# The order of loads, sums and stores at the borders of two node loops in a graph layer (one core)

## Chip, core and metric

One core of a Trainium2 chip runs the whole layer. The metric is device time in microseconds (us), as the median of the runs of one kernel. The engines are PE (TensorE: matmuls and transposes into eight PSUM banks), DVE (VectorE), ACT (ScalarE), POOL (GpSimd) and SP (SyncE, which here only issues transfers). Each engine works through its own list of instructions.

## What is computed

There are 32 batches of 512 tokens with 256 channels, and one 512 x 512 adjacency matrix for each batch.

```python
h = maximum(layernorm(x), 0)
c1 = relu(bn1(conv1(h)));  x_conv = relu(h + bn2(conv17(c1)))      # 1 tap, then 17 taps along the tokens
s = h @ w_se.T + b_se                                                # 3 features of each token
A = exp(-|s_n - s_m|^2) * adj                                        # affinity, masked
msg = relu(h @ w_msg.T + b_msg);  x_nmp = A @ msg
gi = concat(x_conv, x_nmp) @ w_ih.T + b_ih;  gh = h @ w_hh.T + b_hh
r = sigmoid(gi_r + gh_r);  z = sigmoid(gi_z + gh_z);  n = tanh(gi_n + r * gh_n)
out = x + (1 - z) * n + z * h
```

All of it is float32.

## The kernel before

The batches form two groups of 16 (`GB`). Each group passes through two phases, and one late phase follows for all.

- **First phase** (`first_part`): it normalises a batch (`statistics`, `normalise`, which writes `xn`), transposes it (`transpose_h`, which writes `hT`, also stored to memory as `hd`), does the one-tap convolution (`conv1`, which writes `h1`) and turns windows of its result into frequencies (`windows_to_freq`, which writes `xf`). In group 0 the 17-tap weights are turned into frequencies as well and stored as `wd`.
- **Node phase** (`nodes`): it computes the affinity and the messages of every batch of the group, multiplies them, and between these does the frequency products (`product`) of the 17-tap convolution. This is the phase that the change touches.
- **Late phase**: for pairs of batches it goes back from frequencies (`inverse`), computes the gates with combined weights `sw` (`gates_rz`, `gate_n`), and writes the output.

The order of the instructions on every engine, and of the transfers on every queue, is the order in which the Python code makes the calls. Nothing reorders them (`tc.manual_schedule()`); only the waits between engines are put in by the framework, from the buffers that the calls read and write.

In the node phase the batches come in the order `todo`: the last of the group first, since its `hT` is still there, then the others. So group 0 has batches 15, 0, 1, ..., 14 and group 1 has 31, 16, ..., 30. For each batch:

- `load_adj` (L406) issues four transfers of 256 KB on SP; there are two buffers. `load_h` (L413) brings one `hT` of 512 KB back, and `by_chunks` (L424) puts it into another order with two ACT copies; the result is `hq`.
- `message` (L430) is 16 matmuls on PE (L442), with additions on DVE (L444, L445) and a ReLU on ACT. It gives the messages and the three features `st`.
- `features` (L450) writes the matrices `fl` and `fr` with six DVE instructions. `factors` (L460) transposes them on PE into `psl` and `psr` (L463, L468), and ACT copies them to `sl` and `sr`.
- `turn` (L472) transposes adjacency on DVE (L475), in four parts. `exponents` (L479) makes the distances `pd` on PE (L486) and the exponentials on ACT (L488). `masked` (L490) multiplies the two on DVE (L492).
- `aggregate7` (L527) forms the product of messages and affinity with seven half-size products (L538) where a plain one needs eight. For that POOL adds and subtracts blocks: `affinity_sums` (L499, four instructions of 128 x 512, results in `ts`) and `message_sums` (L508, four of 128 x 256, results in `ms`). The second of the seven products reads the third result of the first and the second of the other, called t2 and s2. There is one buffer for `ts` and one for `ms`. The last two batches of group 1 use the plain product (`aggregate`, L517, L522). ACT and DVE collect the result in `nmp`, of which there is one buffer, and `save_nmp` (L560) stores it through ACT's queue.
- `multiply(u)` does the product of frequency unit `u`: `product` (L372, matmuls L390 in three pairs, copies and additions of the result `y`), whose store is put into the list `stores` and sent by the next `flush()`; then `prepare` of unit u + 2, which makes the operands of its third pair with two POOL additions (`wsum`, L357, and `both`, L370); then the load of one further unit (`load_unit`, L351, two transfers on SP). There are three buffers for unit weights. The units are spread over the iterations: two or three in each of group 0, about three in each of the first 13 of group 1, none in the last three of group 1.

Before its loop, `nodes` does the messages, features and affinity of the first batch and the messages and features of the second. An iteration `i` then multiplies batch `todo[i]` with its affinity and gets `todo[i+1]` (`more[0]`), `todo[i+2]` and `todo[i+3]` ready.

Of the kernel before, what the change touches and what calls it, by code (L numbers as in the profile page):

```python
# [15 lines left out]
P = 128  # L16
# [49 lines left out]
def gnn_layer(  # L66
# [283 lines left out]
    def load_unit(g, u, pool=wts):  # L350
        t = WT[g, u] = pool.tile([P, 2, DC, D], FP, tag="wt", name=f"wt_{g}_{u}")  # L351
        for k in range(2):
            nc.sync.dma_start(t[:, k], WD[2 * u + k, : D * D].rearrange("(p i o) -> p i o", i=DC, o=D))
# [52 lines left out]
    def load_adj(b):  # L406
        ADJ[b] = pools["nodes"].tile([P, N // 32, P], FP, tag="adj", name=f"adj_{b}", bufs=2)

        rows = adj[b].rearrange("(j r) (g m) -> g r j m", r=32, g=4)
        for g in range(4):  # L410
            nc.sync.dma_start(ADJ[b][32 * g : 32 * (g + 1)], rows[g])
# [60 lines left out]
    def turn(b, mcs):  # L472
        for mc in mcs:
            at = AT[b, mc] = pools["nodes"].tile([P, N], FP, tag="at", name=f"at_{b}_{mc}", bufs=2)
            nc.vector.transpose(at.rearrange("p (j k) -> p j k", k=32), ADJ[b][:, :, 32 * mc : 32 * (mc + 1)])  # L475
        if NC - 1 in mcs:
            del ADJ[b]
# [36 lines left out]
        nc.gpsimd.tensor_tensor(t[:, 1], a21, a11, op=sub)  # L514
        nc.gpsimd.tensor_tensor(t[:, 2], a12, t[:, 1], op=sub)

    def aggregate(b):  # L517
        NMP[b] = work.tile([P, DC, N], FP, tag="nmp", name=f"nmp_{b}", bufs=1)
        for dc in range(DC):
            p = bank(f"pn_{b}_{dc}")  # L520
            for mc in range(NC):
                nc.tensor.matmul(p, MSG[b][:, mc, dc * P : (dc + 1) * P], A[b][:, mc, :],  # L522
                                 start=(mc == 0), stop=(mc == NC - 1))
            nc.scalar.copy(NMP[b][:, dc, :], p)
        del MSG[b], A[b]

    def aggregate7(b):  # L527

# [471 lines left out]
    with tc.tile_pool(name="freq", bufs=1) as fpool:  # L1000
# [3 lines left out]
        with phase("first", "gen"):  # L1004
            gen = pools["gen"]
            per = N // D
            steps = [partial(weights_to_freq, gen, pc, i) for pc in range(QI // PI) for i in range(0, PI, per)]

            X[0] = pools["first"].tile([P, NC, D], FP, tag="x", name="x_0", bufs=3)
            for c in range(NC):  # L1010
                (nc.sync if c % 2 == 0 else nc.scalar).dma_start(X[0][:, c, :], x[0, c * P : (c + 1) * P, :])
            load_w1()
            load_x(1)
            load_taps(gen, 0, nc.sync)
            nc.scalar.dma_start(taps, nc.inline_tensor(taps_np, name="dft_taps").ap())
            nc.scalar.dma_start(fwd, nc.inline_tensor(fwd_np, name="dft_fwd").ap())

            def between(b):
                if 1 <= b <= len(load_weights):
                    load_weights[b - 1]()  # L1020

                n = (2, 0, *(3 if b in (6, 11) else 2 for b in range(2, GB)))[b]
                mine = [[steps.pop(0)] for _ in range(n)]
                if b % 2 == 0 and b // 2 + 1 < QI // PI:
                    mine[b > 0].insert(0, partial(load_taps, gen, b // 2 + 1))
                return (mine[0], mine[1:]) if b == 0 else mine

            with tc.manual_schedule():
                xf = first_part(0, freq_tile, between)

                for u in range(2):
                    load_unit(0, u)


        LEFT = 4

        def nodes(g, xf, units, last, following=()):


            b1 = (g + 1) * GB  # L1040
            pw = pools["pw"]
            todo = [b1 - 1] + list(range(g * GB, b1 - 1))
            loads = [u for u in (*units, *following) if (g, u) not in WT]
            stores = []

            def load_units(n):
                for _ in range(n):
                    if loads:
                        load_unit(g, loads.pop(0))

            def flush():
                while stores:
                    stores.pop(0)()

            def multiply(u):
                product(pw, g, u, xf, stores)
                if u + 2 in units:
                    prepare(pw, g, u + 2, xf)
                load_units(1)

            load_adj(todo[0])
            load_adj(todo[1])
            load_units(3 - sum((g, u) in WT for u in units))
            load_h(todo[3])
            message(todo[0])
            features(todo[0])
            message(todo[1], [0])
            factors(todo[0])
            message(todo[1], [1])
            turn(todo[0], [0, 1])  # L1070
            features(todo[1])
            exponents(todo[0])
            by_chunks(todo[2])
            masked(todo[0], [0, 1])
            turn(todo[0], [2, 3])
            masked(todo[0], [2, 3])
            affinity_sums(todo[0])
            prepare(pw, g, units[1], xf)
            for i, b in enumerate(todo):
                mine = spread(units, i, last) if i < last else []  # L1080
                more = todo[i + 1 : i + 5]
                seven = i <= last

                if g + 1 < NG and i == GB // 2:
                    load_x(b1)
                if g + 1 < NG and i == 3 * GB // 4:
                    statistics(b1)
                if len(more) > 1:
                    load_adj(more[1])
                if len(more) > 3:  # L1090
                    load_h(more[3])
                if seven:
                    message_sums(b)
                if more:
                    factors(more[0])
                flush()
                for u in mine[:1]:
                    multiply(u)
                if len(more) > 1:
                    message(more[1])  # L1100
                    flush()
                    features(more[1])
                if more:
                    turn(more[0], [0, 1])
                    exponents(more[0])
                    masked(more[0], [0, 1])
                for u in mine[1:2]:
                    multiply(u)
                if more:
                    turn(more[0], [2, 3])  # L1110
                    masked(more[0], [2, 3])
                if seven:
                    aggregate7(b)
                else:
                    aggregate(b)
                if more and i + 1 <= last:
                    affinity_sums(more[0])
                flush()
                for u in mine[2:]:
                    multiply(u)  # L1120
                save_nmp(b)
                if len(more) > 2:
                    by_chunks(more[2])
            flush()

        with phase("pw", "ahead"):
# [103 lines left out]
```

## Time and profile before

| | |
|---|---|
| Median of 3 runs | 1826.45 us (1826.16 to 1829.45) |
| The profiled execution | 1826.99 us |
| Its span, from the first to the last instruction | 1825.1 us |
| PE matmuls / weight loads, busy | 98% / 63% |
| DVE / POOL / ACT, busy | 66% / 43% / 34% |
| First phase of group 0 | to 156 us |
| Node phase of group 0 | 156 to 451 us |
| First phase of group 1 | 451 to 566 us |
| Node phase of group 1 | 566 to 859 us |
| Late phase | 859 us to the end |

The page gives busy times of the engines over the span; "granted clock" is the share of its full rate at which PE ran. A wait has the form "engine line waited for: us in total, times, longest", and in a timeline the brackets hold the idle time of the engine before the instruction and what ended it. A waiting instruction is named by the line of the call that issued it. DMA queues bear the name of the engine that issues on them.

### The profile page before, as it was taken

To read this page: it belongs to the slowest core of one execution; us is meant where nothing else is said; L and a number is where in the kernel's file an instruction comes from. 1 tells how busy PE (TensorE), PEld (TensorE's weight loads), DVE (VectorE), ACT (ScalarE), POOL (GpSimd) and SP (SyncE) were. 2 spreads that over 40 slices of the span, in tenths; PEclk is the share of its full clock that TensorE was granted. 3 is DMA by queue.
4 is the path that set the end of the run, shared out by engine and by line. 5 is a ranking of instruction groups with operands and counts; after the bars stand their busy time and mean duration, and the time that the engine had idled before them with its cause. 6 is when DMAs were issued, how large, how long until landed. Compare 5 with 4: busy or idle time off the path is not lost.

```text
span 1825.1 us, 21215 instructions
## 1 busy us (share of the span) xinstructions
PE 1793.3 (98%) x6974; PEld 1152.5 (63%) x6974; DVE 1203.6 (66%) x2370; ACT 617.9 (34%) x1252; POOL 781.1 (43%) x731
## 2 busy tenths in 40 slices
PE   9998999999999999999999999999999999999998
PEld 6776778887998888886545554555445554555444
DVE  7874877876896778774266556664666456655666
ACT  4554444443445444443212221222212221222121
POOL 3431787777433877776421332223231323133221
PEclk9998999999999999999999999999999999999999
DMA  9999786885668887888342244224422443234412
GB/s 260 309 293 226 209 243 202 247 222 175 218 231 214 238 240 233 235 227 269 81 119 69 55 121 121 87 35 121 121 89 40 114 121 101 54 88 121 117 21 53
DMA packets 308657, 289.32 MB, mean 159 GB/s; under 512 B 148076, under 2 KB 238732, under 8 KB 308164
## 3 DMA queue, kind: packets, MB, share of 16 engines
q1 hardware_dynamic: 282964, 225.79, 46.7%
q10 hardware_dynamic: 18992, 38.68, 6.0%
q0 software_dynamic: 6592, 23.50, 4.1%
q8 instruction: 56, 0.92, 0.2%
q14 instruction: 53, 0.43, 0.1%
HBM read 191.50 MB, written 96.40 MB: 158 GB/s over the span
## 4 chain that ended last, share of the span: by engine, by line
PE 92%; DVE 2%; POOL 2%; issue 2%; DMA 1%; ACT 0%; SPq 0%; ACTq 0%; DVEq 0%; POOLq 0%
PE pg L664 30%; PE pn L664 15%; PE py L390 11%; PE pn L538 9%; PE pm L442 6%; PE pc L326 6%; PE pc L652 5%; PE px L341 3%; PE pd L486 2%; PE pw L254 2%; PE phT L310 1%; DMA adj<-in_adj_dram 1%; PE pn L522 1%; PE pz L664 1%; PE psr L468 1%
## 5 line engine op out<-in xcount | busy, mean ns | idle before, releaser
L642 POOL TENSOR_TENSOR hp<-hp 128x512 f32<-128x512 f32 x64 | 80.5, 1269 | 415.1 <-DMA hp<-hd 352.3
L664 PE MATMUL pg<-hp,sw 128*128 128x512 f32 x434 | 221.8, 593 | 1.1 <-DVE u L695 0.6
L664 PE MATMUL pg<-np,sw 128*128 128x512 f32 x434 | 221.6, 592 | 0.0
L664 PE MATMUL pg<-cp,sw 128*128 128x512 f32 x434 | 221.6, 592 | 0.0
L642 POOL TENSOR_TENSOR cp<-cp 128x512 f32<-128x512 f32 x64 | 80.6, 1269 | 225.0 <-ACT cp L658 223.7
L390 PE MATMUL py<-wt,xf 128*128 128x256 f32 x640 | 157.0, 389 | 0.0
L679 ACT ACTIVATE rz<-rz,brz 128x512 f32<-128x512 f32 x93 | 67.0, 721 | 260.2 <-DVE rz L683 260.2
L664 PEld LDWEIGHTS pg<-hp,sw 128*128 128x128 f32 x434 | 82.2, 190 | 105.1 <-issue 97.4
L664 PEld LDWEIGHTS pg<-np,sw 128*128 128x128 f32 x434 | 82.5, 190 | 103.8 <-issue 103.8
L664 PEld LDWEIGHTS pg<-cp,sw 128*128 128x128 f32 x434 | 82.5, 190 | 103.8 <-issue 103.8
L357 POOL TENSOR_TENSOR wsum<-wt 128x512 f32<-128x512 f32 x78 | 107.6, 1380 | 83.3 <-DMA wt<-wd 57.7
L390 PEld LDWEIGHTS py<-wt,xf 128*128 128x128 f32 x640 | 118.6, 193 | 35.4 <-issue 21.2
L803 ACT ACTIVATE nt<-nt,vech 128x512 f32<-128x512 f32 x64 | 46.2, 722 | 236.5 <-DVE nt L802 236.5
L442 PE MATMUL pm<-wmsg,hq 128*128 128x259 f32 x512 | 119.1, 385 | 1.9 <-ACT hq L427 1.9
L326 PE MATMUL pc<-w,hT 128*128 128x256 f32 x512 | 117.7, 383 | 0.9 <-DVE hT L314 0.9
L664 PE MATMUL pn<-cp,sw 128*128 128x512 f32 x224 | 114.4, 592 | 0.0
L664 PE MATMUL pn<-np,sw 128*128 128x512 f32 x224 | 114.4, 592 | 0.0
L664 PE MATMUL pn<-hp,sw 128*128 128x512 f32 x224 | 114.4, 592 | 0.0
L326 PEld LDWEIGHTS pc<-w,hT 128*128 128x128 f32 x512 | 94.6, 190 | 23.9 <-issue 5.6
L492 DVE TENSOR_TENSOR A<-A,at 128x512 f32<-128x512 f32 x128 | 108.2, 882 | 1.9 <-ACT A L488 1.9
L442 PEld LDWEIGHTS pm<-wmsg,hq 128*128 128x128 f32 x512 | 97.0, 191 | 19.0 <-ACT hq L427 4.0
L652 PEld LDWEIGHTS pc<-back,yt 128*128 128x128 f32 x640 | 92.7, 190 | 7.7 <-issue 7.7
(169 smaller groups left out, 3379.1 us busy)
## 6 DMA issues: line engine op xcount, KB each, us to landing
wt<-wd SPq DMA_DIRECT2D x160, 256.0 KB, 4.9
adj<-in_adj_dram SPq DMA_DIRECT2D x128, 256.0 KB, 6.7
wd<-wst SPq DMA_DIRECT2D x64, 320.0 KB, 5.5
yd<-y ACTq DMA_DIRECT2D x80, 256.0 KB, 4.5
yt<-yd SPq DMA_DIRECT2D x30, 640.0 KB, 7.5
hd<-hT SPq DMA_DIRECT2D x32, 512.0 KB, 5.0
nd<-nmp ACTq DMA_DIRECT2D x32, 512.0 KB, 4.7
xb<-in_x_dram SPq DMA_DIRECT2D x128, 128.0 KB, 3.7
```

The lines of the kernel that those rows point to most:

```text
L326: nc.tensor.matmul(p[:, j, :], HT[b][:, ic, c * P : (c + 1) * P], w1[:, ic, :], start=(ic == 0), stop=(ic == DC - 1))
L341: nc.tensor.matmul(p[:, j * 2 * L : (j + 1) * 2 * L], H1[b][:, c0 + j, ic * P : (ic + 1) * P], fwd, start=True, stop=True)
L357: nc.gpsimd.tensor_tensor(t, WT[g, u][:, 0], WT[g, u][:, 1], op=ALU.add)
L390: nc.tensor.matmul(dst, v[:, ic, :], w[:, ic, :], start=(ic == 0), stop=(ic == DC - 1))
L442: nc.tensor.matmul(p[:, : D + NS], hq[:, ic, c * P : (c + 1) * P], wmsg[:, ic, :], start=(ic == 0), stop=(ic == DC - 1))
L492: nc.vector.tensor_mul(A[b][:, mc, :], A[b][:, mc, :], AT.pop((b, mc)))
L538: nc.tensor.matmul(bk, left[:, k, :], right[:, k, :], start=(first and k == 0), stop=(k == 1), skip_group_check=True)
L642: nc.gpsimd.tensor_tensor(t[:, dst, :], t[:, a, :], t[:, b, :], op=sub)
L652: nc.tensor.matmul(bk[:, t0:t1], YT[p][j][:, c, oc * P : (oc + 1) * P], back[:, n : n + t1 - t0], start=(c == 0), stop=(c == len(spans) - ...
L664: nc.tensor.matmul(bk[:, t], sw[:, k, q, o, :], terms[k][q][:, t], start=(first and i == 0), stop=(i == len(ks) - 1), skip_group_check=True)
L679: nc.scalar.activation(rz[:, g, j, :], src, AF.Sigmoid, bias=brz[:, g : g + 1], scale=1.0)
L803: nc.scalar.activation(n, n, AF.Tanh, bias=b_in[:, i : i + 1], scale=1.0)
```

## The change

- The loads of units 0 and 1 leave the end of group 0's first phase. `nodes` now issues the adjacency of its first batch, then three unit loads (in group 1 they are loaded already), then the second adjacency.
- Ahead of the loop, `message_sums` of the first batch comes right after its features; the features of the second batch and the exponentials of the first come before the first `turn`; `prepare` of the second unit comes before `affinity_sums`.
- In an iteration, `message_sums` of the next batch comes just before its `affinity_sums`, at the end, and no longer at the top of the iteration after. `by_chunks` moves from the end to the place after the exponentials. `save_nmp` is not called at once but put into `stores`, to be sent by the next `flush()`.
- In the first iteration alone, the message of batch `todo[2]` and its features (`bring`) come before the product of unit 0.
- In the last iteration, all units that are left are multiplied before the aggregation.
- A plain aggregation is split: its first half comes ahead of the next batch's `turn` and exponentials.

```diff
--- before.py
+++ after.py
@@ -514,15 +514,17 @@
         nc.gpsimd.tensor_tensor(t[:, 1], a21, a11, op=sub)
         nc.gpsimd.tensor_tensor(t[:, 2], a12, t[:, 1], op=sub)
 
-    def aggregate(b):
-        NMP[b] = work.tile([P, DC, N], FP, tag="nmp", name=f"nmp_{b}", bufs=1)
-        for dc in range(DC):
+    def aggregate(b, dcs=range(2)):
+        if 0 in dcs:
+            NMP[b] = work.tile([P, DC, N], FP, tag="nmp", name=f"nmp_{b}", bufs=1)
+        for dc in dcs:
             p = bank(f"pn_{b}_{dc}")
             for mc in range(NC):
                 nc.tensor.matmul(p, MSG[b][:, mc, dc * P : (dc + 1) * P], A[b][:, mc, :],
                                  start=(mc == 0), stop=(mc == NC - 1))
             nc.scalar.copy(NMP[b][:, dc, :], p)
-        del MSG[b], A[b]
+        if DC - 1 in dcs:
+            del MSG[b], A[b]
 
     def aggregate7(b):
 
@@ -1028,9 +1030,6 @@
             with tc.manual_schedule():
                 xf = first_part(0, freq_tile, between)
 
-                for u in range(2):
-                    load_unit(0, u)
-
 
         LEFT = 4
 
@@ -1059,27 +1058,34 @@
                 load_units(1)
 
             load_adj(todo[0])
+            load_units(3 - sum((g, u) in WT for u in units))
             load_adj(todo[1])
-            load_units(3 - sum((g, u) in WT for u in units))
             load_h(todo[3])
             message(todo[0])
             features(todo[0])
+            message_sums(todo[0])
             message(todo[1], [0])
             factors(todo[0])
             message(todo[1], [1])
-            turn(todo[0], [0, 1])
             features(todo[1])
             exponents(todo[0])
             by_chunks(todo[2])
+            turn(todo[0], [0, 1])
             masked(todo[0], [0, 1])
             turn(todo[0], [2, 3])
             masked(todo[0], [2, 3])
+            prepare(pw, g, units[1], xf)
             affinity_sums(todo[0])
-            prepare(pw, g, units[1], xf)
             for i, b in enumerate(todo):
                 mine = spread(units, i, last) if i < last else []
                 more = todo[i + 1 : i + 5]
                 seven = i <= last
+
+                def bring():
+                    if len(more) > 1:
+                        message(more[1])
+                        flush()
+                        features(more[1])
 
                 if g + 1 < NG and i == GB // 2:
                     load_x(b1)
@@ -1089,22 +1095,24 @@
                     load_adj(more[1])
                 if len(more) > 3:
                     load_h(more[3])
-                if seven:
-                    message_sums(b)
                 if more:
                     factors(more[0])
                 flush()
+                if i == 0:
+                    bring()
                 for u in mine[:1]:
                     multiply(u)
-                if len(more) > 1:
-                    message(more[1])
-                    flush()
-                    features(more[1])
+                if i > 0:
+                    bring()
+                if not seven:
+                    aggregate(b, [0])
                 if more:
                     turn(more[0], [0, 1])
                     exponents(more[0])
+                    if len(more) > 2:
+                        by_chunks(more[2])
                     masked(more[0], [0, 1])
-                for u in mine[1:2]:
+                for u in mine[1:2] if more else mine[1:]:
                     multiply(u)
                 if more:
                     turn(more[0], [2, 3])
@@ -1112,15 +1120,15 @@
                 if seven:
                     aggregate7(b)
                 else:
-                    aggregate(b)
+                    aggregate(b, [1])
+                flush()
+                stores.append(partial(save_nmp, b))
                 if more and i + 1 <= last:
+                    message_sums(more[0])
                     affinity_sums(more[0])
-                flush()
-                for u in mine[2:]:
-                    multiply(u)
-                save_nmp(b)
-                if len(more) > 2:
-                    by_chunks(more[2])
+                if more:
+                    for u in mine[2:]:
+                        multiply(u)
             flush()
 
         with phase("pw", "ahead"):
```

## Prediction

> **What bounds the kernel now.** I read the page's busy row first: TensorE (PE) is busy 98% of the span, so only its 32 us of holes, and the stretches at half clock that follow holes, can be won. The chain of waits confirms it (PE 92%). Next, PE's own waits:
>
> ```profile
> PE       1793.3 (98%) x6974; PEld 1152.5 (63%) x6974; DVE 1203.6 (66%) x2370; ACT 617.9 (34%) x1252; POOL 781.1 (43%) x731
> ```
>
> ```profile
> PE psl L463 <- DVE fl L456: 11.6, 2, 8.9
> PE pn L538 <- POOL ms L514: 3.5, 3, 2.2
> PE pm L442 <- ACT hq L427: 1.9, 3, 1.0
> ...
> PE pd L486 <- ACT sr L470: 1.2, 1, 1.2
> ```
>
> These four rows lie in the node loops, nearly all at their borders: 18.2 us. Between the borders PE has no wait. The timeline of the first entry shows the largest one (start us, us, engine, operation, wait in brackets):
>
> ```profile
> 163.73 1.14 PE L486 MATMUL pd<-sr,sl 9*128 9x512 f32 x8
> 164.90 2.05 ACT L488 ACTIVATE A<-pd 128x512 f32<-128x512 f32 x4
> 166.81 1.16 ACT L427 COPY hq<-hT 128x512 f32<-128x512 f32 x2
> 172.16 1.30 DVE L475 STREAM_TRANSPOSE at<-adj 128x512 f32<-128x512 f32 x2 [7.83 <-DMA adj<-in_adj_dram]
> 173.78 0.48 PE L463 MATMUL psl<-ident,fl 128*128 128x128 f32 x1 [8.91 <-DVE fl L456]
> 174.95 3.62 PE L390 MATMUL py<-wt,xf 128*128 128x256 f32 x8
> ```
>
> The adjacency lands at 172.0; `turn` waits for it on DVE; batch 0's `features`, behind `turn` on DVE, come after; PE's transposes of them (`factors`) last of all. The eight product matmuls after it take 3.6 us, elsewhere 1.9: the granted clock is 0.50 from 168.7 to 178.9. At the ends of the loops:
>
> ```profile
> 438.80 0.72 POOL L512 TENSOR_TENSOR ms<-msg 128x256 f32<-128x256 f32 x1
> 441.18 1.55 PE L538 MATMUL pn<-ts,ms 128*128 128x256 f32 x4 [2.15 <-POOL ms L514]
> 448.15 1.89 PE L390 MATMUL py<-wt,xf 128*128 128x256 f32 x8
> 448.69 1.38 DVE L302 TENSOR_SCALAR xn<-x,mv,rstd 128x256 f32<-128x256 f32 x4
> ```
>
> ```profile
> 842.77 1.14 PE L486 MATMUL pd<-sr,sl 9*128 9x512 f32 x8 [1.16 <-ACT sr L470]
> 843.84 15.70 PE L522 MATMUL pn<-A,msg 128*128 128x512 f32 x32
> 847.42 1.47 POOL L619 DMA_DIRECT2D np<-nd x2 [11.34 <-DVE at L475]
> ```
>
> To see here: at group 0's end PE waits for POOL, then product 35 (448.15) covers DVE's `xn` for the next phase. At group 1's end a 1.2 us wait is followed by a clock of 0.50 from 844.5, and POOL fetches `np` for the gates only after the last `turn`.
>
> [...] drops at 168.7, 441.75, 578.3 and 844.5 us are all whole multiples of 3.41 us apart, and a hole of 2.15 us, even one of 1.16 us among transposes and short matmuls, was enough. [...] SP waited 3.1 us for `wd` writes ahead of unit 0, and so of the adjacency.
>
> **First entry (group 0).** SP: today `load_h` (issued 155.5 to 156.6), four unit loads (159.9 to 161.6), four adjacency loads (161.7 to 163.5), four more (to 170.5). The change puts adjacency 15 first: four issues of 0.49 from 156.6 on; its memory was last read by batch 14's windows, done at 153.9. With today's slowest landing, 7.9, it is there by 166 instead of 172. Six unit issues follow from 159.7; landing in 5.1 they are there by 168. Adjacency 0 is issued to 166 and lands by 175 (9.3), `hT` of batch 2 by 176 (9.1); `by_chunks` asks for it at 177.9.
>
> PE: `features(0)` no longer stands behind `turn(15)`, so after 164.87 the transposes run at once, 0.55, to 165.4. Next now is `message(1)`, not product 0. It needs `hq`: ACT ends the exponentials at 166.95 and the first copy at 167.4. PE starts at 167.5, a **new wait of 2.1 us**. [...] I take a half-clock window, +1.7. Message 3.65 + 1.7 to 172.9, product 0 1.9 to 174.8, `pd` 1.07, product 1 2.75 to 178.6, `aggregate7` 6.04 to 184.7; today 192.8. Gain 8.1. Inputs: DVE turns and masks in 5.2 to 171.1; POOL has t2 after three of its 1.3 us steps, at 175.0, before PE asks at 179.5, since message sums (3.2) and `prepare(1)` (2.0) are ahead and done by 170. In iteration 1 the 0.96 us wait on `hq` goes, `by_chunks` being early and ACT no longer waiting for the store. **−9.1**; bounds −10.9 (no cold window) and −6.5 (loads 2 us later than I have them).
>
> **Steady loop.** Same instructions; message sums and affinity sums swap on POOL, 13.5 us of POOL work in 16.5 us; `by_chunks` (1.16 on ACT) comes before the copies of the second product, where PE's banks leave about 1 us; the `nmp` store goes out some 0.8 us later. Zero, hidden by PE.
>
> **End of group 0.** From `aggregate7(13)`'s end at 418.7 POOL is a solid chain: message sums 3.2 (from 417.8, when the old ones are read), affinity sums 5.5, prepare 33 and 34 5.1, to 431.6; sums again 8.7; prepare(35) 2.0, to 442.3. The 0.84 us wait in `aggregate7(14)` goes. But product 35 now stands ahead of `aggregate7(15)`, and `prepare(35)` behind both sums: PE reaches its third part at 438.7 and waits 3.6 us. Then 0.9 + 6.0 + 1.2 for the cold clock: 450.4. And `xn` has lost its cover: it follows the last `nmp` additions on DVE, so the transposes wait about 1.6 and end at 452.9, today 451.6. **+1.3**; bounds −1 and +3.5.
>
> **Second entry (group 1).** The weights are loaded already. Today PE waits 2.68, then runs cold; after: transposes to 574.8, `hq` at 576.8 (ACT 576.19 plus one copy), a wait of 2.0. Message and product 0 end at 584.0 with a cold window, 582.4 without; today 584.7. I take **−1.2**; bounds −2.9 and +0.5.
>
> **End of group 1.** The 1.16 us wait (ACT stood at the `nmp` store) is covered by half an aggregation, and the cold window (32 matmuls in 15.7 instead of 13.8) goes: −2.9. Against it: the exponentials of batch 30 now follow an ACT copy that waits for the deferred store of the single `nmp` buffer: issued 842.3, landing in 5.4 at 847.7, copy to 848.3, exponentials from there (today 844.0). The last mask then comes about 0.9 too late for PE, and the last `turn` moves from 847.1 to 851.5. POOL's `np` loads, sums (10.4) and the five late `sw` parts follow that: issued from 865.3, landing in 8.7 or less, needed at 873.4; +0.5. **−1.5**; bounds −3 and +2.
>
> **Sum:** −9.1 + 1.3 − 1.2 − 1.5 = −10.5. The profiled execution took 1826.99 us, its span 1825.1; 1814.6 of span, 1816.5 with the 1.9 around it. The median shown, 1826.45, is 0.5 lower: 1816.0.
>
> **Rivals.**
> (1) *The adjacency stays late* (crowded queues: the DMA share is above 1 from 162 on). At 172.0 again, DVE holds message(1)'s bank reads to 177.3 and PE stops at `pd`; `aggregate7(15)` starts at 181.7, not 178.6. With later weights up to 4 us lost: 1819.5. For it: adjacency lands in up to 9.3 us; against it: it would be issued 5 us earlier into a queue with one `hT` load and four writes.
> (2) *The short new waits leave the clock up* and the end of group 0 is free: 1812. [...]
> (3) *The ends cost more*: product 35 and `xn` +3.5, late `sw` +3: 1821.
> (4) *Slower.* The deferred store holds the one `nmp` buffer; the next `aggregate7` needs it about 11.1 us after the store's issue (403.5 to 414.6 in one steady iteration). Stores land in 2.6 to 6.6 us. If they took over 11.1, each of some 29 iterations would stop, and from 11.5 on (10.5/29 more) the whole gain is gone; at 12 the time is 1842.
> (5) *The order of one queue undoes it all*: no change, 1826.
>
> **Numbers.** 0.2% of the time, 3.7 us, is about what a measurement can tell. Main case 45%, (2) 20%, (1) 13%, (3) 14%, (4) 4%, (5) 4%. Faster by more than 0.2%: 0.92; within: 0.04; slower: 0.04. The range reaches to (2) and (3): 1811 to 1821.5.
>
> **What would show it.** Right: the wait of psl on fl gone from PE's list; pm on hq about 2 us at each entry; `py` on POOL's `both` near 3.6 us at group 0's end, then phT on xn; pd on sr gone. `aggregate7(15)` ends near 185. Wrong: PE waiting for `adj` through DVE in the first entry, for unit weights, for `nd` stores within the loop, or pg on `sw` for more than 2 us.

## The result and the profile after

The changed kernel took 1826.24 us (median of 4 runs, 1824.04 to 1830.52), the kernel before in the same runs 1827.95 (4 runs). The ratio is 0.9993, with a 95% interval from 0.9971 to 1.0016: no change that can be measured. The forecast of 1816.0 (1811.0 to 1821.5) was wrong. The profiled execution of the changed kernel took 1826.73 us, its span 1825.0 (before: 1826.99 and 1825.1). One execution of each was profiled, so a small difference between two stages can be chance; the table below shows beside it what other executions of the same code took.

First PE's waits in the kernel after (engine, line, waited for, us in total, times, longest). Lines from `aggregate` on are two higher than before, so L538 is now L540 and L664 is L666:

```profile
PE py L390 <- POOL both L370: 4.4, 2, 4.2
PE pm L442 <- ACT hq L427: 3.8, 2, 1.9
PE pg L666 <- DMA sw<-ws: 2.8, 2, 2.2
PE pn L540 <- ACT p L545: 2.8, 1, 2.8
...
PE phT L310 <- DVE xn L302: 0.9, 1, 0.9
PE pn L523 <- DVE A L492: 0.9, 2, 0.5
```

The four rows shown of before (psl on fl 11.6, pn on ms 3.5, three waits of pm on hq, pd on sr 1.2) are gone. In their place stand 15.6 us of other waits, two of them for ACT's `hq` again, now in one piece at each entry. Three were forecast (py on both, pm on hq, phT on xn); pn on p was not, and pg on sw was forecast as next to nothing.

Where the time went, in us, from the timelines. A stage ends with the last matmul named, or with the start of what it runs "to"; the boundary runs from the first matmul of `inverse(0)` to that of `inverse(1)`. Positions were rounded to 0.1 first, so a stage can be 0.1 off. The last column has the same stages in those kernels of the experiments below whose code is the same there: first the one that shares it with the kernel before, then those that share it with the kernel after.

| Stage | before | after | after - before | same code, other kernels |
|---|---|---|---|---|
| first phase of group 0, to the first message | 156.1 | 156.6 | +0.5 | 155.9; 155.8 to 158.6 |
| message(15) to the end of the first `aggregate7` | 36.9 | 32.7 | -4.2 | 37.3; 31.1 to 32.4 |
| to the end of the second `aggregate7` | 17.8 | 16.5 | -1.3 | 17.9; 16.6 to 18.5 |
| to the end of `aggregate7` in iteration 13 | 208.0 | 206.4 | -1.6 | 207.0; 206.3 to 208.2 |
| to the first transpose of group 1 | 31.9 | 34.2 | +2.3 | 30.2; 34.1 to 35.6 |
| first phase of group 1, to message(31) | 114.8 | 116.4 | +1.6 | 114.8; 115.3 to 116.7 |
| message(31) to the end of its `aggregate7` | 29.2 | 26.9 | -2.3 | 30.1; 26.9 to 28.4 |
| loop of group 1, to `inverse(0)` | 264.7 | 263.6 | -1.1 | 264.7; 262.9 to 264.6 |
| boundary, to `inverse(1)` | 41.7 | 47.9 | +6.2 | none; 48.0 |
| the rest of the late phase | 924.0 | 923.8 | -0.2 | 923.9; 923.6 to 923.7 |

So in these two executions 10.7 us were gained and 10.6 lost again. The two entries, the end of group 0, the first phase of group 1 and the boundary differ by more than executions of the same code do. The first phase of group 0, the second `aggregate7` and the loop of group 0 do not, and the loop of group 1 hardly does: these rows can't be told from chance. The chain of waits was no help in finding the losses: it gives PE 71% of the span and no other engine more than 1%. The stage table and the timelines at each border show them.

**First entry.** The timeline of the kernel after:

```profile
168.01 3.85 PE L442 MATMUL pm<-wmsg,hq 128*128 128x259 f32 x16 [1.92 <-ACT hq L427]
170.33 3.82 SPq L415 DMA_DIRECT2D hT<-hd  x1
181.95 1.14 ACT L427 COPY hq<-hT 128x512 f32<-128x512 f32 x2 [3.02 <-DMA hT<-hd]
183.54 0.37 ACT L545 COPY p<-pn 128x256 f32<-128x256 f32 x1
183.96 2.07 PE L540 MATMUL pn<-A,msg 128*128 128x256 f32 x4 [2.77 <-ACT p L545]
```

`features(0)` runs at once and the 8.9 us wait is gone. But the `hT` of the fourth batch is issued at 170.3, lands at 181.9, and ACT, which now does `by_chunks` ahead of the copies of the aggregate, stands 3.0 us for it. PE waits 2.8 us for the copy of p, which stands behind it on ACT, and runs on a slower clock after it (2.07 us for four matmuls that take 1.03 elsewhere; the granted clock is 0.50 from 183.8 to 187.2).

**End of group 0.** Product 35's third part waits 4.19 us for POOL, and then the transposes for DVE:

```profile
436.82 2.08 PE L390 MATMUL py<-wsum,both 128*128 128x256 f32 x4 [4.19 <-POOL both L370]
438.69 1.60 PE L540 MATMUL pn<-A,msg 128*128 128x256 f32 x4
446.39 1.64 PE L310 MATMUL phT<-ident,xn 128*128 128x128 f32 x8 [0.93 <-DVE xn L302]
```

**Boundary.** The chain of the late `sw`, engine by engine:

```profile
843.75 0.59 ACT L525 COPY nmp<-pn 128x512 f32<-128x512 f32 x1 [6.15 <-DMA nd<-nmp]
844.87 1.29 DVE L492 TENSOR_TENSOR A<-A,at 128x512 f32<-128x512 f32 x2 [6.76 <-ACT A L488]
847.68 1.47 POOL L621 DMA_DIRECT2D np<-nd  x2 [16.45 <-DVE at L475]
861.07 1.61 POOL L608 DMA_DIRECT2D sw<-ws  x3
870.82 1.12 PE L666 MATMUL pg<-np,sw 128*128 128x512 f32 x2 [0.59 <-DMA sw<-ws]
874.16 2.07 PE L666 MATMUL pg<-cp,sw 128*128 128x512 f32 x2 [2.21 <-DMA sw<-ws]
876.02 1.91 PE L666 MATMUL pg<-hp,sw 128*128 128x512 f32 x2
```

The first copy of the split aggregate waits until the `nmp` store has landed; the exponentials, the mask and the last `turn` come behind it; POOL fetches `np` after that `turn` and `sw` 13.4 us later. In the kernel before POOL fetched `np` at 847.42, and `sw` so:

```profile
860.81 1.61 POOL L606 DMA_DIRECT2D sw<-ws  x3
```

So `sw` leaves at the same time, while PE has come 6.1 us earlier. The windows show the clock behind the holes (window, length, busy us and count of PE, PEld, DVE, ACT, POOL, granted clock, DMA share, GB/s):

```profile
866.60:870.00 3.40, 3.40 (x9) 1.33 (x7) 1.21 (x2) 0.00 (x0) 3.32 (x4) 1.00 1.07 376
870.00:873.40 3.40, 1.36 (x3) 0.30 (x2) 0.17 (x1) 0.00 (x0) 3.32 (x4) 0.99 1.09 310
873.40:876.80 3.40, 2.64 (x3) 1.17 (x4) 0.00 (x0) 0.53 (x1) 3.24 (x3) 0.50 0.13 15
876.80:880.20 3.40, 3.40 (x5) 1.33 (x4) 0.00 (x0) 0.15 (x1) 1.34 (x2) 0.51 0.00 0
```

PE is busy 1.36 of 3.40 us, and the clock is at half for the next 6.8. The waits are 2.8 us and half of 6.8 is 3.4: together about the 6.2 of the table.

### The profile page after: what moved, and what is told of

It is laid out like the page before. It is cut to its first block, busy times and chain, and to the rows that moved or that the text cites. A ratio compares the mean times of both kernels' runs of the same rounds, so it can differ in the third digit from the quotient of the medians.

```text
span 1825.0 us, 21270 instructions
## 1 busy us (share of the span) xinstructions
PE 1796.4 (98%) x6974; PEld 1152.0 (63%) x6974; DVE 1236.8 (68%) x2370; ACT 621.9 (34%) x1252; POOL 782.6 (43%) x731
## 4 chain that ended last, share of the span: by engine, by line
PE 71%; POOL 1%; issue 1%; DMA 1%; DVE 1%; ACT 0%; DVEq 0%; POOLq 0%; ACTq 0%
PE pg L666 29%; PE pn L666 15%; PE py L390 6%; PE pn L540 5%; PE pc L654 5%; PE pm L442 3%; PE pc L326 3%; PE px L341 2%; PE phT L310 1%; PE pd L486 1%; PE pz L666 1%; DMA sw<-ws 1%; DMA nd<-nmp 0%; PE psr L468 0%; POOL hp L644 0%
## 5 line engine op out<-in xcount | busy, mean ns | idle before, releaser
L666 PE MATMUL pg<-cp,sw 128*128 128x512 f32 x434 | 223.0, 595 | 2.2 <-DMA sw<-ws 2.2
L666 PE MATMUL pg<-hp,sw 128*128 128x512 f32 x434 | 222.7, 595 | 0.7 <-DVE rz L685 0.5
L666 PE MATMUL pg<-np,sw 128*128 128x512 f32 x434 | 222.6, 594 | 0.6 <-DMA sw<-ws 0.6
L666 PEld LDWEIGHTS pg<-cp,sw 128*128 128x128 f32 x434 | 82.9, 191 | 106.9 <-issue 103.6
L666 PEld LDWEIGHTS pg<-np,sw 128*128 128x128 f32 x434 | 82.7, 191 | 105.3 <-issue 103.9
L666 PEld LDWEIGHTS pg<-hp,sw 128*128 128x128 f32 x434 | 82.5, 191 | 105.5 <-issue 98.8
L666 PE MATMUL pn<-hp,sw 128*128 128x512 f32 x224 | 114.4, 592 | 0.0
L666 PE MATMUL pn<-cp,sw 128*128 128x512 f32 x224 | 114.4, 592 | 0.0
L666 PE MATMUL pn<-np,sw 128*128 128x512 f32 x224 | 114.4, 592 | 0.0
```

Source lines behind the costliest of these rows:

```text
L666: nc.tensor.matmul(bk[:, t], sw[:, k, q, o, :], terms[k][q][:, t], start=(first and i == 0), stop=(i == len(ks) - 1), skip_group_check=True)
```

## The experiments

Every ratio is against the kernel before, run on the same chip beside it; its medians there were 1828.4 to 1828.7 us. "After" stands for the changed kernel, 0.9993 (0.9971 to 1.0016). That interval is about 4 us to either side, so a kernel that lies 4 or 5 us from "after" is told from it by the stage in question, not by its median alone.

### The late transfer of sw, from both sides

First `sw` alone is issued early:

```diff
         load_combined(sw, 0, 2)
+        load_combined(sw, 2, 7)
         sums(HP[0], True)
         sums(NP[0], False)
-        load_combined(sw, 2, 7)
```

> The kernel after, with one change: POOL issues the second transfer of the masked sums (sw, products 2 to 6) right after the first one, ahead of the sums of the projections, instead of behind them and the last sums of the aggregates. Theory L (late sw): in the kernel after, TensorE came to the boundary after the node loops 6.1 us earlier than in the kernel before and lost 6.3 us there, because this transfer is issued at 861.07 us whatever TensorE does. Issued early, it lands before 870 us: the waits of pg on sw (0.59 and 2.21 us) and the cold matmuls behind them go, inverse(1) starts at about 895.5 instead of 901.4, and the time is about 6 us below the kernel after, 1820. Rival F (fixed later clock: what is gained ahead of 860 us is taken back later by transfers of the later stages that do not come sooner): inverse(1) starts earlier but the end stays at 1825, time within 1.5 us of the kernel after. Rival N (the waits on sw are only where other lateness shows): the waits move to another operand of the same stage and inverse(1) stays at 901.

Measured: 1821.6 us, ratio 0.9965 (0.9953 to 0.9977). The boundary took 41.9 us instead of 47.9, and from `inverse(1)` to the end 923.7. The waits on `sw` are gone, though `np` still waits for the last `turn`. `inverse(1)` began at 898.8, not at about 895.5 as expected, because the profiled execution came to the boundary 3.7 us later than that of the kernel after, with the same code up to there. The timeline of this kernel:

```profile
851.34 1.47 POOL L621 DMA_DIRECT2D np<-nd  x2 [16.65 <-DVE at L475]
852.80 3.21 POOL L608 DMA_DIRECT2D sw<-ws  x6
```

That last stretch was 923.6 to 924.0 us long in all fourteen kernels, whatever stood ahead of it. So no later clock takes gains back: rival F falls, and so does N.

Second, the cause of the lateness. The plain aggregates are not split:

```diff
-                if not seven:
-                    aggregate(b, [0])
...
-                    aggregate(b, [1])
+                    aggregate(b)
```

> The kernel after, with one change: the plain aggregates of the last batches aren't split in halves; both stand at their old place, behind the turn. Theory S (it is the half moved ahead of the exponents that makes sw late: its first copy on ScalarE stands 6.2 us until the nmp store has landed, the exponents, the last turn, np and sw queue behind it): the last turn starts at about 840 instead of 846, POOL issues sw at about 855 instead of 861, and the waits of pg on sw go. TensorE reaches the boundary later by 1 to 2 us (35.1 us from the last aggregate7 to inverse(0) in the kernel before, 33.4 in the kernel after), so inverse(1) starts 4 to 5 us earlier than in the kernel after, time about 1822. Rival D (the deferred store itself is what is late, split or not): the copy of the whole aggregate waits as long, sw stays at 861, time within 1.5 us of the kernel after.

Measured: 1823.8 us, 0.9969 (0.9958 to 0.9981). The boundary took 41.7 us. The timeline of this kernel:

```profile
840.57 1.29 DVE L492 TENSOR_TENSOR A<-A,at 128x512 f32<-128x512 f32 x2 [1.39 <-ACT A L488]
843.37 1.47 POOL L621 DMA_DIRECT2D np<-nd  x2 [11.12 <-DVE at L475]
856.75 1.61 POOL L608 DMA_DIRECT2D sw<-ws  x3
```

Without the split, DVE waits 1.4 us for the exponentials and not 6.8, and the whole chain comes 4.3 us sooner, while PE comes to the boundary at 853.6, as after (853.3). The store is still deferred here, so rival D falls: it is the half aggregation ahead of the exponentials that made `sw` late. Nor is there a sign that the split pays ahead of the boundary: the loop of group 1 took 262.5 us without it, and 262.9 to 264.6 in the executions with it.

Third, a control, the kernel before with `sw` early:

> Control: the kernel before with only the sw transfer early. Theory L: in the kernel before that transfer lands 1.6 to 5.8 us ahead of its use, so issuing it early changes nothing, time within 2 us of the kernel before. Rival: the early issue is a gain in itself (it would take 4 to 6 us off the kernel before too), and then the gain seen in the kernel after says nothing about what the change had made late.

Measured: 1830.3 us (22 runs), 1.0009 (0.9998 to 1.0020). The early issue gains nothing where `sw` was in time; in the changed kernel it repairs what the change had made late.

### The end of group 0

The last iteration multiplies its further units behind the aggregate again:

```diff
-                for u in mine[1:2] if more else mine[1:]:
+                for u in mine[1:2]:
                     multiply(u)
...
-                if more:
-                    for u in mine[2:]:
-                        multiply(u)
+                for u in mine[2:]:
+                    multiply(u)
```

> The kernel after, with one change: in the last iteration of a group the products of the unit beyond the second go behind the aggregate again, as in the kernel before, instead of ahead of it. Theory X (the end of a group lost because product 35 came ahead of POOL's prepare): the wait of py on POOL's both (4.19 us at 436.8) and the phT wait on xn (0.93) go or shrink to under 1 us, and the stretch from aggregate(13) to the first phT of group 1 is 3 to 4 us shorter than in the kernel after (35.9 us there, 32.9 before). The time of the whole kernel falls by that only if the late sw transfer, issued at 861 us, doesn't take it back: with theory L of the late sw, the time stays within 1.5 us of the kernel after, although message(31) starts 3 us earlier. Rival: the wait belongs to prepare itself, which is late on POOL in either order; then the wait only moves behind the aggregate and message(31) starts within 1 us of the kernel after.

Measured: 1821.8 us, 0.9966 (0.9954 to 0.9979). The stretch to the first transpose of group 1 took 29.3 us instead of 34.2, less than in the kernel before (31.9, and 30.2 in the control above). Its timeline has neither wait:

```profile
437.20 1.13 PE L540 MATMUL pn<-ts,ms 128*128 128x256 f32 x4 [1.79 <-POOL ts L505]
442.48 1.89 PE L390 MATMUL py<-wt,xf 128*128 128x256 f32 x8
445.07 1.04 PE L310 MATMUL phT<-ident,xn 128*128 128x128 f32 x8
```

Product 35, at 442.48, finds its operands ready and covers `xn`, as it did before. Half of this expectation fell: I had thought that the late `sw` would take the gain back. It did not. The boundary was as long as after (48.0 us, waits on `sw` 3.9), but the loss there is a length, not a fixed time on the clock, since `sw` follows the last `turn`, and `turn` moves with PE.

Both edits together:

> The kernel after with two edits: the sw transfer early and the last unit behind the aggregate. Apart they measured 1821.6 and 1821.8 us, each with the rest of the kernel after unchanged. Theory (two separate losses, one of 6 us after 859 us, one of 4 to 5 us before the first transpose of group 1): they add, inverse(1) starts at about 894 and the time is about 1817. Rival (the two gains are one: with sw off the path, the earlier end of group 0 meets another cap): time stays at 1821 to 1822.

Measured: 1815.3 us (1814.45 to 1816.89), **0.9929 (0.9917 to 0.9941)**. The two gains add (4.6 and 4.4 us of median apart, 10.9 together, which is the sum within the noise), the stretches are 29.3 and 41.7 us. This kernel beats both, and it is the fastest median of the study, though the last kernel of the next section comes within 0.9 us of it. It is the change with its two losses taken out, and it comes out at the time that was forecast for the change.

### The first entry

The features are loaded ahead of the second adjacency:

```diff
-            load_adj(todo[1])
             load_h(todo[3])
+            load_adj(todo[1])
```

> The kernel after, with one change: at the entry of a group the features of the fourth batch are loaded ahead of the adjacency of the second, not behind it. Theory H (the entry gained only half of its forecast because these features landed at 181.8 and ScalarE stood 3.0 us for them in the middle of the first iteration): ScalarE's hq wait on hT at 181.95 goes, with it the 2.77 us wait of pn on p at 183.96 and the slow matmuls after it; aggregate7(15) ends 3 to 4.5 us earlier, at 185 to 186 instead of 189.1, and aggregate7(13) does too. The time of the whole kernel: within 1.5 us of the kernel after by theory L (the late sw takes it back), 4 lower without it. Rival A: the adjacency of the second batch is then late by the same amount and VectorE's masks for it hold TensorE; aggregate7(15) ends within 1 us of 189.1.

Measured: 1840.7 us, 1.0067 (1.0055 to 1.0079). What theory H said of the first `aggregate7` held: it ended at 185.9, 28.0 us after the message began (after: 32.7, before: 36.9), and ACT did not wait for `hT`. But the second one then took 26.4 us (after: 16.5), a loss that neither expectation had. In group 1 it is 26.0 us for 19.2. The waits of SP's own queue, and then the timeline:

```profile
SPq L415 <- DMA yd<-y: 6.0, 1, 6.0
```

```profile
187.13 0.34 SPq L415 DMA_DIRECT2D hT<-hd  x1
187.57 1.80 SPq L353 DMA_DIRECT2D wt<-wd  x4
193.94 1.28 POOL L357 TENSOR_TENSOR wsum<-wt 128x512 f32<-128x512 f32 x1 [11.17 <-DMA wt<-wd]
204.66 2.08 PE L540 MATMUL pn<-ts,ms 128*128 128x256 f32 x4 [6.26 <-POOL ts L505]
```

A load of features waits 6.0 us for a store of products, although they share no data; the unit loads stand behind it on SP, POOL's `prepare` waits 11.2 us for the weights, and the sums `ts` come behind `prepare`. The times show the tie: the store of product 0 was issued at 184.27 and landed at 187.07, and the load went out at 187.13, although the Python code calls the load first. So there are waits beside those that come from the buffers. In the kernel after, the same load goes out at 181.94, 0.06 us after an earlier `hT` load has landed (181.88), and 5 us sooner. The views give the pairs and their times, not what ties them.

Moving `by_chunks` back to the end of the iteration, with the loads as after, hits the same tie:

```diff
                     exponents(more[0])
-                    if len(more) > 2:
-                        by_chunks(more[2])
                     masked(more[0], [0, 1])
...
+                if len(more) > 2:
+                    by_chunks(more[2])
```

> The kernel after, with one change: by_chunks, ScalarE's copies of the features, at the end of each iteration again, not in its middle. Theory C (ScalarE stood 3.0 us for late features at 181.95 because by_chunks had been moved ahead): the 2.77 us wait of pn on p at 183.96 goes, aggregate7(15) ends 3 to 4 us earlier, at about 185.5. In the steady loop the waits of pm on hq, three of them and 1.9 us in all in the kernel before, come back if the place of by_chunks had removed them (rival Q: they stay away because the deferred store had removed them). Time: gain 3 to 4 at the entry less 2 to 3 in the loop, 1824 to 1827, by itself hardly to be told from the kernel after; the stage positions decide.

Measured: 1841.9 us, 1.0069 (1.0057 to 1.0081). The first `aggregate7` ended at 186.0 and the second was late by the same stop (5.8 us on `ts`): the load of features, on SP, waited 7.2 us for a store of products. So the forecast of time was off by 15 us. The loop has no wait of pm on hq, so the place of `by_chunks` is not what removed those. That is half of rival Q; its other half, that the deferred store removed them, comes up again below.

All three edits together:

> The three edits together: features of the fourth batch ahead of the second adjacency, the last unit behind the aggregate again, and the sw transfer early. Theory (gains at the entries and in the loops are real and were lost at three places, the last of which caps all that comes before it): the gains add up now that the cap is off, 6 + 3.5 + 4 = 13 us, time about 1813, inverse(1) starts at about 888. Rival F (fixed later clock): the end stays within 2 us of the kernel after whatever stands ahead of 900 us. Rival P (partial): a transfer later than sw becomes the cap, and the sum stops at about 6 to 8, time 1818 to 1820.

Measured: 1830.0 us, 1.0008 (1.0000 to 1.0016). The end of group 0 took 29.3 us and the boundary 41.6, as in the run that combines only these two, while the second `aggregate7` took 26.8. None of the three expectations was right: the gains of two edits are there and the third costs 14 to 15.

Then the tie itself was tried, which is theory R: the load of features is held by the store of product 0. First the store of product 0 is only issued sooner (`flush()` ahead of the second product in iteration 0, on top of the three edits):

```diff
+                if i == 0:
+                    flush()
                 for u in mine[1:2]:
                     multiply(u)
```

> The three edits of the run with 1830.0 us (features of the fourth batch first, last unit behind the aggregate, sw early) and one more: in the first iteration of a group the store of the first product is issued ahead of the second product, not behind the aggregate. Theory R ([...] POOL's prepare and with it the sums ts come late, and TensorE stops 6.3 us in aggregate7(0)): with the store issued 4 us sooner the load goes out at about 184 instead of 187, the stop falls from 6.3 to 2 to 3.5 us at each entry, time about 1822 to 1824. Rival B (the adjacency of the second batch, loaded later, is what is late): the stop stays at 6 us, time 1830. Rival P (POOL's order alone makes ts late): the same, 1830.

Measured: 1820.9 us, 0.9957 (0.9944 to 0.9970). The store landed at 184.21 and the `hT` load went out at 184.27, forecast 184; the stop fell from 6.3 to 4.1 us in group 0, less than forecast (2 to 3.5), and is gone in group 1. Rivals B and P, which had no change here, fall as the only cause. Second, the same store leaves through POOL's queue:

```diff
-        store = partial(nc.scalar.dma_start, YD[g][:, 2 * u : 2 * u + 2, :], y)
+        store = partial((queue or nc.scalar).dma_start, YD[g][:, 2 * u : 2 * u + 2, :], y)
...
                 for u in mine[:1]:
-                    multiply(u)
+                    multiply(u, nc.gpsimd if i == 0 else None)
```

> As the run before it (features first, last unit behind the aggregate, sw early, first store early), but the store of the first product of each group's first iteration goes through POOL's queue[...]. Theory R: the next load of features then waits for no store, goes out at about 181, the unit loads behind it follow at 182, prepare and ts are in time: the stop of pn on ts falls from 6.3 us to under 1.5 at both entries, the early end of aggregate7(15) (186) is kept, time 1812 to 1815. Rival B or P: stop and time as in the run with 1830.0 us.

Measured: 1818.3 us, 0.9950 (0.9935 to 0.9965). The timeline of this kernel:

```profile
178.29 1.06 SPq L415 DMA_DIRECT2D hT<-hd  x1
179.63 10.21 SPq L353 DMA_DIRECT2D wt<-wd  x4
188.91 1.26 POOL L357 TENSOR_TENSOR wsum<-wt 128x512 f32<-128x512 f32 x1 [7.45 <-PE pm L442]
198.76 1.13 PE L540 MATMUL pn<-ts,ms 128*128 128x256 f32 x4 [3.38 <-POOL ts L505]
```

The load is free of the store (178 instead of 187), as theory R says, and with the earlier issue it makes 12 us less than the three edits alone. But 3.4 us of stop stay, where I expected under 1.5: POOL now starts `prepare` at 188.9 and needs 9.8 us for it, the message sums and three steps of the affinity sums, in that order. The trace puts POOL's wait down to a message matmul of PE, with which `prepare` shares no data. What ended just before is a transfer: the second half of the unit's weights landed at 188.74, and `prepare` started 0.17 us later. In three other kernels (after, features first, and the next one) it starts 0.16 to 0.17 us after that landing too. And this second half left 2.6 us behind the first, at 182.27, after SP had waited 2.3 us for a part of an adjacency, with which it shares no data and which had landed at 182.26. So a tie of this kind is in this wait as well. That POOL does `prepare` and the message sums ahead of the affinity sums (rival P) adds its 9.8 us behind the weights; no run here has another order.

Last, the copies for the second message ahead of the exponentials:

```diff
-            exponents(todo[0])
             by_chunks(todo[2])
+            exponents(todo[0])
```

> As the run before it, and by_chunks of the third batch ahead of the exponents of the first at the entry, so that ScalarE's copies for the second message come first. Theory: the two waits of pm on hq at the entries (1.9 us each) go or shrink to under 0.5 us, 3 to 4 us less than the run before it, about 1809 to 1812. Rival: the exponents, now 1.2 us later, hold the masks and the sums ts of the first batch, and the aggregate waits for them as long: time within 1.5 us of the run before it.

Measured: 1816.2 us, 0.9939 (0.9924 to 0.9954), 2.1 below the run before it with intervals that overlap, so neither the forecast (3 to 4 less) nor its rival (within 1.5) is decided. The two waits of pm on hq (3.8 us) went. In group 1 the stretch from the message to the end of `aggregate7` fell from 28.6 to 26.1 us; in group 0 the first `aggregate7` ended later (31.4 us for 28.2), and the second at 205.5 for 204.2. From message(15) to the end of the second `aggregate7` this kernel took 47.9 us, the run before it 48.4, the kernel after 49.2, the kernel before 54.7. The four other kernels with the entry of the kernel after took 47.7 to 49.9 over the same stretch, so of all that was tried at the first entry nothing brought more than the changed kernel that could be told from chance.

### The entry alone

The kernel before with only the order of loads and work at the entries, and the message sums ahead of the affinity sums:

> Only the entry of the change: the order of loads and of work at the entry of a group and the message sums ahead of the affinity sums as in the kernel after, everything inside the iterations (features, split aggregate, store, by_chunks, the last unit) as in the kernel before. Theory (the entries gain and the ends lose): the gains at the two entries stay, about 4 to 8 us at the first and 2 at the second, none of the losses at the ends is there (sw issued before 856, product 35 behind the aggregate), so the time is 6 to 9 us below the kernel before, 1818 to 1822. Rival W (the entry needs the moves inside the iteration: with the second message ahead of the features the wait for late loads comes back there): the first entry gains under 2 us and the time is within 2 us of the kernel before.

Measured: 1833.6 us, 1.0032 (1.0019 to 1.0045). Slower, against both expectations. The first `aggregate7` gained 7.5 us (29.4 us for 36.9), the second lost 6.3 (24.1 for 17.8), and in the loop pm waits for hq again, 1.8 and 1.6 us, and ACT's `sr` holds pd for 2.0. This kernel and the one with `by_chunks` late have that copy in the same place; the second has the deferred store and no such wait. That points to the deferred store as what removed the loop's waits (1.0 us in the kernel before); the two kernels differ in other points too, so it is not shown. Behind the entry SP's adjacency loads waited up to 12.2 us for an `nmp` store. In these runs an early end of the first `aggregate7` was thus no gain in itself: it lasted only where the loads of the next iteration came as early.

## Why the prediction was wrong, step by step

- **First entry, -9.1: the failed step is "`hT` of batch 2 by 176".** It landed at 181.9, as late as in the kernel before (181.5). It was issued at 170.3, not 166.9, and took 11.5 us to land, not 9.1. I had let SP issue one transfer after the other, where this one went out only when a unit load, with which it shares no data, had landed: that was issued at 163.5 and landed at 170.26, and the `hT` load went out at 170.33. With `hT` in time the first `aggregate7` does gain 8.9 (the run with the features first); with the tie it does not last. Measured for the step, with the wait in iteration 1: -5.5. Up to the aggregate the path was right, psl without a wait and a wait of 1.92 on hq (2.1 forecast), and the start of the aggregate at 178.4 (178.6) was right partly by luck. The half clock that I took behind the wait, an estimate from the drops in the trace of the kernel before, did not come (message(1) took 3.85 us, not 5.35), but adjacency 15 landed at 168.4, not 166, so DVE's masks ended at 174.2, not 171.1, and the `pd` matmuls, whose banks DVE empties behind the masks, took 2.30 us, not 1.07; and the message of batch 15 had begun 0.5 later.
- **Steady loop, 0.** The -1.6 of the table can't be told from chance. What is there: the loop of group 0 had two waits on hq, 0.68 us at 266.9 and 0.28 at 352.8, which the prediction overlooked ("Between the borders PE has no wait"), and no kernel with the deferred store has them.
- **End of group 0, +1.3.** The mechanism was right: py on both 4.19 us (3.6 forecast), phT on xn 0.93 (1.6 forecast). The size was off: +2.3 here, and +1.6 more in the first phase of group 1, which I hadn't costed. With the product back behind the aggregate the end is 4.9 us shorter, but 0.7 of the 1.6 remain (115.5 us, and 115.2 to 115.5 in all six kernels with this edit); the cause of that rest is open.
- **Second entry, -1.2.** Measured -2.3: of my two cases the one with the clock up came. That was luck. Ten kernels have the same wait of 1.9 us on hq there. In three of them (after, the one with two edits, the one with `by_chunks` late) the clock stays up and the stage takes 26.9 us; in the seven others it falls to half, and the stage takes 28.3 to 29.7. The kernel after, and the one without the split:

```profile
574.24 3.85 PE L442 MATMUL pm<-wmsg,hq 128*128 128x259 f32 x16 [1.92 <-ACT hq L427]
```

```profile
574.20 5.30 PE L442 MATMUL pm<-wmsg,hq 128*128 128x259 f32 x16 [1.92 <-ACT hq L427]
```

- **End of group 1, -1.5: the mis-sized term is the landing of `sw`.** PE's part was forecast as -2.0 (-2.9, and 0.9 for the last mask). From the end of the last `aggregate7` to `inverse(0)` it measured -1.5 (18.3 us before, 16.8 after), with the 0.9 us of waits for masks; the rest I didn't trace. The chain of the late `sw` was right: I had its issue moved by 4.5 us against the PE work ahead of this end, measured 4.9. Then I let it land "in 8.7 or less" and allowed 0.5. The three transfers of that kind landed in 7.1, 9.2 and 12.0 us; in the kernel before the same three had taken 8.7, 10.8 and 13.5, and I had taken the first of them for all. The views of `sw`, before and after:

```profile
DMA to landing us min/median/max: 8.7/10.8/13.5
```

```profile
DMA to landing us min/median/max: 7.1/9.2/12.0
```

The second and the last set the waits, 2.8 us in two holes, and behind those came a half clock that I had priced at every other border and left out here: 6.2 instead of 0.5. Here a stretch in which PE was busy for 1.36 of 3.40 us was followed by 6.8 us at half clock.

Of the rivals, (3), the ends cost more, named the right two places and gave 3 and 3.5 us; with 6.2 and 3.9 it would have come to 1824. Rival (5), no change, came true in its number. Of its reason, the order of one queue, only a part holds: SP's queue took back some 4 us of the first entry, and the boundary and the end of group 0 took the rest. The forecast was not far from what the change is worth without its two losses: 1815.3 measured, 1816.0 forecast. That agreement is in part luck, since the terms differ and the kernel before measured 1828.4 beside it: the gain is 13 us, where 10.5 were forecast.

## What to carry to other kernels

Cost a transfer at the end of its chain by its slowest landing (12.0 us here, for 7.1 of the first), not by a typical one, and allow for a half clock behind every hole that it makes (6.8 us of it here, behind holes of 0.6 and 2.2 us). Before moving work ahead of other work on the same engine, list what it waits for: three of the losses here (ACT on `hT`, 3.0 us; PE on `prepare`, 4.2 us; the exponentials on the `nmp` store, 6.2 us) are each a moved instruction that waits with others queued behind it. Where a load goes out only when a transfer without common data has landed, as here (0.06 us behind it), find that transfer in the trace before moving the load. When a change bundles several moves, undo each alone: here two of its parts cost what the others gained.

## What the runs showed of the hardware and the program

- With the features first, a 512 KB load on SP's queue waited 6.0 us for a store on ACT's queue without common data and went out 0.06 us after that had landed, at 187.1; this one change in the order cost 14 us in all (1840.7 after 1826.2). With all three edits and the store issued sooner the load went out at 184.3, and with that store also sent through POOL's queue at 178.3.
- DVE's masks and POOL's sums, both with two 128 x 512 operands, took longer when they ran at once: in the run with POOL's store two mask steps took 2.59 us instead of 1.25 (DVE, 193.64) while POOL's sums took 1.73 and 1.60 instead of 1.27. Over the whole trace of the kernel after, the median mask step took 0.67 us with no POOL work beside it (53 of them) and 1.22 with POOL busy for over four fifths of it (43).
- Two holes of 0.6 and 2.2 us were followed by 6.8 us at half clock, worth about 3.4 us, although PE was busy for 2.64 of the first 3.40 us of these.
- The same hole of 1.9 us, at the second entry, was followed by a half clock in seven of ten kernels, at 1.4 us or more each (28.3 to 29.7 us for 26.9), and by none in three. In the kernel after, the half clocks ahead of PE's last matmul begin at 183.83, 436.42 and 873.32, whole multiples of 3.413 us apart, and last 3.4, 3.4 and 6.8 us.
